# Graph layer with FFT convolution, one core: where the first four filter kinds of a batch are put, and when they are loaded

## The chip, the cores and the metric

The kernel runs on one core of a Trainium2 chip. The metric is the device time of one execution in microseconds (us). The engines are named as in the profile: PE multiplies matrices (PEld is its loading of weights, which overlaps), DVE is the vector engine, ACT the scalar engine, POOL the GpSimd engine, and SP the engine whose queue issues most of the DMA transfers. All times below are of this kernel's runs or of one profiled execution of it.

## The reference, cut to what matters

There are 64 graphs of 256 nodes with 256 features each. One layer is computed:

```python
h = relu(layernorm(x))                       # x: 64 x 256 x 256
xc = transpose(h)                            # channels x nodes
c = relu(bn1(conv1d(xc, conv1_w)))           # width 1
c = bn2(conv1d(c, conv2_w))                  # width 17, padded by 8
x_conv = transpose(relu(c + xc))
s = h @ w_se.T + b_se                        # 3 values per node
A = exp(-dist(s, s)) * adj
x_nmp = A @ relu(h @ w_msg.T + b_msg)
out = x + GRU(input=[x_conv, x_nmp], state=h)   # 256 features, gates r, z, n
```

The change concerns the filter of the convolution of width 17.

## The kernel before, in words

**Batches and pairs.** The 64 graphs are worked on as 32 pairs; four pairs make a batch, so there are eight batches (`NB`). In the loop over `b`, `i` is the first pair of the batch that is finished and `nxt` the first of the next one, which is prepared at the same time.

**The convolution.** The convolution of width 17 is done in a transformed domain. The transform of four pairs is made on DVE (`split`, `forward`), into tiles `U`, `V`, `PT`, `Sv`. In that domain the filter is 47 matrices of 256 x 256 numbers, called kinds here; a kind is named by a point `n` and a number 0, 1 or 2 (`TURNS` is their order). They are computed once, in the first batch, and written to device memory (`filt`). Every batch loads all 47 again, 256 KB each, into tiles `wb` of SBUF, of which there are nine (`SLOTS`). `product` takes the kind that stands first in the deque `WB` and issues four matmuls of 128 x 128 by 128 columns with it. `begin(m)` does the two products of number 0 for two points and has ACT copy the sum to the other half of the PSUM accumulator; `complete(m)` adds the products of numbers 1 and 2, and ACT copies the results to `Yv` or `Yu` (which is `V`). DVE then transforms back (`branch_back`, `odd_back`, `q_back`, `p_back`, `join`).

**Slots.** `free` holds the numbers of the free slots, `pending` the kinds still to load, and `load_kinds` pairs them, one DMA on SP's queue for each kind. After a product its slot goes back to `free` and new loads are recorded. When all 47 kinds are used, all nine slots are free; `roles` then takes all nine of them as work tiles for the gates (`ah`, `axn`, `axc`, `bh`, `bxn`, `bxc` for sums of operands, `e` for a partial product, `tz0` and `tz1` for the gate z). At the end of the batch seven come back by `give`, and `load_kinds` records the first seven loads of the next batch; `tz0` and `tz1` come back a little later in the next batch.

**The gates.** `gates(i)` does the GRU of one pair with `seven`, a product of 2 x 2 blocks by seven multiplications, once for the gates r and z and once for the two halves of gate n, with the function `between` recorded between the two. A batch has four gates, of `i` to `i + 3`, and the last ones run just ahead of the first products of the next batch. In the last gates the message of pair `nxt` (`message`, matmuls `aux<-w_msg,hT`, a DVE addition, small ACT copies to `Z`) is woven in. `embed` transposes `Z` on PE, and nine small ACT copies bring the result to `zT`. `affinity` makes the matrix A from it.

**The tiles concerned.** `adjh` (512 KB) takes the adjacency of a pair from device memory by four DMAs (`load_adj`); `join_adj` has ACT copy it to `adj_rows` in two instructions, one for each half of every number, after which `adjh` stands empty until the next `load_adj`. `xnms` is a ring of two tiles of 512 KB each; `aggregate(i)` writes one of them, and the gates of pair `i` read it last. `hh` and `halves` are the tiles through which the next pairs' `h` is transposed by DMA (`turn_h`, `sort_h`, `join_h`).

**What sets the order.** Every instruction is recorded (`Recorder`), with its dependences found from the elements that it reads and writes. `plan` then orders all engines' queues by a list schedule with costs and due times of its own, and `emit` issues them in that order. So the place where a call is written in the loop is not where its instruction stands in its engine's queue: a load is issued as soon as the planner thinks fit, once its tile's last reader is done. All instructions have the line of the recording helper, 371, in the profile; they are told apart by the names of their tiles, `out<-in`.

Of the kernel before, what the change touches and what calls it, by code (L numbers as in the profile page):

```python
# [13 lines left out]
FP = mybir.dt.float32  # L14
# [472 lines left out]
def kernel(  # L487
# [20 lines left out]
    B, N, D = x.shape  # L508
# [3 lines left out]
    NB = B // GB  # L512
    NP = B // G
    DC = D // P
# [26 lines left out]
    def keep(name, *dims):  # L541
        return const.tile([P, *dims], FP, name=name)
# [26 lines left out]
    SLOTS = 9  # L569
    WARM = 21  # L570
    slots = [keep(f"wb{k}", DC, D) for k in range(SLOTS)]
# [8 lines left out]
    adjh = keep("adjh", 2 * MC * W // 2).bitcast(U16).rearrange("p (k w) -> p k w", w=W)  # L580
# [59 lines left out]
    def join_adj(i):  # L640
        if not BY_DMA <= i < NP:
            return
        v = adj_rows.bitcast(U16).rearrange("p (g c) (n j) -> p j c g n", g=G, j=2)
        u = adjh.rearrange("p (c j) (g n) -> p j c g n", j=2, g=G)
        for j in range(2):
            nc.scalar.copy(v[:, j], u[:, j])
# [75 lines left out]
    p = aux()  # L722
# [175 lines left out]
    free = deque(range(SLOTS))  # L898
# [3 lines left out]
    def load_kinds(count=SLOTS):  # L902
        for _ in range(count):
            if not (free and pending):
                return
            n, kind = pending.popleft()
            WB.append((free.popleft(), n, kind))
            m, k = PLACE[n, kind]
            nc.sync.dma_start(out=slots[WB[-1][0]], in_=filt[m][:, k])


    def operands(n):
        if n < 8:
            c, h = n // 2 % 2, n // 4 * 2 + n % 2
            return Sv(c, h), V(c, 4 + h), V(c, h)
        if n < 12:
            c, h = (n - 8) // 2, n % 2
            return U(c, 4 + h), U(c, h), U(c, 2 + h)
        if n < 14:
            return U(n - 12, 6), PT(n - 12, 2), PT(n - 12, 3)  # L920
        if n == 14:
            return U(0, 7), PT(0, 1), PT(1, 1)
        return U(1, 7), PT(1, 0), None
# [3 lines left out]
    def product(p, n, kind, start):  # L927
        k, a, b = WB.popleft()
        assert (a, b) == (n, kind)
        for o in range(DC):  # L930
            for c in range(DC):
                mm(p[:, (n % 2 * DC + o) * P:(n % 2 * DC + o + 1) * P], slots[k][:, c, o * P:(o + 1) * P],
                   operands(n)[kind][:, c::DC, 0, :], start=start and not (o or c), stop=c == DC - 1,
                   skip_group_check=True)
        free.append(k)
        load_kinds(2)

    def begin(m):

        p = OPEN[m] = acc()  # L940
        for n in (2 * m, 2 * m + 1):
            product(p[:, 0], n, 0, n % 2 == 0)
        nc.scalar.copy(p[:, 1], p[:, 0])

    def complete(m):

        p = OPEN.pop(m)
        for kind in (1, 2):
            for n in (2 * m, 2 * m + 1):
                if operands(n)[kind] is not None:  # L950
                    product(p[:, 2 - kind], n, kind, False)
        re, im = (p[:, c].rearrange("p (n a e) -> p a n e", n=2, e=NW) for c in range(2))
        if m < 4:
            nc.scalar.copy(Yv(m % 2, m // 2 * 2, 2), re)
            nc.scalar.copy(Yv(m % 2, 4 + m // 2 * 2, 2), im)
        elif m < 6:
            nc.scalar.copy(Yu(m - 4, 0, 2), re)
            nc.scalar.copy(Yu(m - 4, 2, 2), im)
        elif m == 6:
            t = Yu.t[:, :, :, 6:8, :].rearrange("p a c n e -> p n a c e")  # L960
            nc.scalar.copy(t[:, 0], re)
            nc.scalar.copy(t[:, 1], im)
        else:
            nc.scalar.copy(Yu(0, 5)[:, :, 0], re[:, :, 0])
            nc.scalar.copy(Yu(1, 5)[:, :, 0], im[:, :, 0])
            nc.scalar.copy(Yu(1, 4)[:, :, 0], re[:, :, 1])
            nc.scalar.mul(Yu(0, 4)[:, :, 0], im[:, :, 1], 0.5)
# [14 lines left out]
    def message(i):  # L982
        if i >= NP:
            return
        for g in range(G):
            for c in range(MC):
                p = aux()
                for k in range(DC):
                    mm(p[:, :D + SE], chunk(HT[i][:, k], g, c), w_msg[:, k, :], start=(k == 0), stop=(k == DC - 1))
                nc.vector.tensor_add(msg_tile[:, g, c], p[:, :D + SE], b_msg)  # L990
        s = msg_tile[:, :, :, D:]
        flat = s.rearrange("p g c s -> p (g c) s")
        nc.scalar.mul(Z[:, 0, :, :SE], flat, -2.0)
        nc.scalar.activation(Z[:, 0, :, SE:2 * SE], flat, AF.Square)
        nc.scalar.copy(Z[:, 1, :, :SE], flat)
        nc.scalar.activation(Z[:, 1, :, 2 * SE:KD], flat, AF.Square)
        for g in range(G):
            nc.scalar.activation(msg_tile[:, g, :, :D], msg_tile[:, g, :, :D], AF.Relu)
# [179 lines left out]
    def gates(i, between=None):  # L1178
# [43 lines left out]
        if between:  # L1222
            between()
# [97 lines left out]
    for b in range(NB):  # L1321
# [26 lines left out]
        if b == 0:  # L1348
# [4 lines left out]
            xnms = Ring(late.tile([P, DC, W], FP, name=f"xnm{k}") for k in range(2))  # L1353
# [60 lines left out]
        def between():  # L1414
            affinity(i + 2)
            join_h(nxt + 1)
            stats(nxt + 2)
        gates(i, between)
        finish(i)
        for n in IN:  # L1420
# [10 lines left out]
        def between():  # L1431
            join_h(nxt + 2)
            join_adj(i + 3)
            message(i + 3)
            stats(nxt + 3)
        gates(i + 1, between)
        finish(i + 1)
        for n in IN:
# [29 lines left out]

        def between():
            join_adj(nxt)  # L1470
        gates(i + 3, between)
        message(nxt)
        if b == NB - 1:
# [50 lines left out]
```

## Time and profile before

| what | value |
|---|---|
| runs | 1688.8, 1692.25, 1693.15 us; median 1692.25 us |
| profiled execution | 1694.44 us, its span 1692.7 us |
| granted PE clock | 0.995 |
| busy, share of the span | PE 98%, PEld 84%, DVE 86%, ACT 67%, POOL 13% |
| loads `wb<-filt` | 376, 256 KB each, on SP's queue |
| loads `adjh<-halves_d` | 112, 128 KB each, on SP's queue |
| DMA moved in all | 261.37 MB, 154 GB/s over the span |

A timeline line gives the start in us, how long the merged group lasts, the engine, the operation with its tiles, the shape and the count of records, and in brackets the idle time ahead of it and what ended it. One matmul of this kernel's 4-byte numbers shows as two records on PE. SPq lines are the issues of DMAs by SP's queue.

### The profile page before, as it was taken

Reading aid. Unit: us, or ns where it says so; the run is one execution under the profiler, and the core shown is the slowest. Engines: PE = TensorE matmul, PEld = TensorE weight load, DVE = VectorE, ACT = ScalarE, POOL = GpSimd, SP = SyncE. Lnnn points to the kernel's source line nnn. Section 1 sums busy time; section 2 is a strip of 40 time slices with the busy share of each in tenths; the row PEclk is TensorE's granted clock in tenths of the full one; section 3 lists DMA queues with packets and bytes.
Section 4 is the critical chain, followed back from the end, with each engine's and each line's share of the span. In section 5 each row is a group of like instructions: output and inputs, shape, how many; then the busy total and the mean of one; then the engine's idle time right before and its main releaser. Section 6 shows DMA issues by size and latency. Waiting matters only on the chain.

```text
span 1692.7 us, 26271 instructions
## 1 busy us (share of the span) xinstructions
PE 1662.7 (98%) x8984; PEld 1420.2 (84%) x8984; DVE 1458.6 (86%) x3401; ACT 1133.6 (67%) x2029; POOL 227.9 (13%) x245
## 2 busy tenths in 40 slices
PE   9999999999999999999999999999999999999997
PEld 6888878988889788888889887898888978898886
DVE  7978989798898998898988988979988989789545
ACT  5545776686767767677665877578576776667554
POOL 4211010022010121102110031002211022000010
PEclk9999999999999999999999999999999999999999
DMA  9981566856568365784458645684646846376032
GB/s 240 304 275 61 128 123 160 276 138 128 111 199 235 94 131 112 229 210 97 116 119 270 166 97 117 159 270 111 142 109 204 225 100 131 82 237 144 13 58 55
DMA packets 314936, 261.37 MB, mean 154 GB/s; under 512 B 192875, under 2 KB 240263, under 8 KB 314802
## 3 DMA queue, kind: packets, MB, share of 16 engines
q1 hardware_dynamic: 297010, 216.71, 48.5%
q0 software_dynamic: 17376, 42.66, 11.2%
q8 instruction: 71, 1.16, 0.3%
q14 instruction: 63, 0.52, 0.1%
q10 hardware_dynamic: 416, 0.32, 0.1%
HBM read 156.60 MB, written 43.78 MB: 118 GB/s over the span
## 4 chain that ended last, share of the span: by engine, by line
PE 64%; DVE 29%; DMA 4%; issue 2%; ACT 2%; SPq 0%; DVEq 0%; ACTq 0%
PE acc L371 44%; PE aux L371 20%; DVE V L371 6%; DVE T L371 4%; DVE tr L371 4%; DVE U L371 3%; DVE wb L371 3%; DMA wb<-filt 3%; DVE gn L371 2%; DVE acc L371 2%; DVE Yv L371 1%; DVE PT L371 1%; DVE st L371 1%; DVE msg L371 1%; DMA hh<-halves 1%
## 5 line engine op out<-in xcount | busy, mean ns | idle before, releaser
L371 PE MATMUL acc<-wb,w_ih 128*128 128x256 f32 x768 | 191.9, 379 | 0.0
L371 PEld LDWEIGHTS acc<-wb,w_ih 128*128 128x128 f32 x768 | 146.0, 190 | 19.7
L371 POOL DMA_DIRECT2D back<-in_x_dram x62 | 56.8, 1056 | 750.8 <-ACT back L371 717.5
L371 POOL TENSOR_TENSOR rstd<-rstd,neg_half 128x4 f32<-128x4 f32 x32 | 84.8, 2650 | 455.4 <-DVE shift L371 266.4
L371 PE MATMUL aux<-wb,w_x 128*128 128x256 f32 x576 | 139.9, 384 | 2.5 <-ACT e L371 2.3
L371 PE MATMUL acc<-wb,w_x 128*128 128x256 f32 x576 | 136.2, 382 | 5.3 <-DVE acc L371 5.3
L371 DVE SCALAR_TENSOR_TENSOR V<-T,V 128x128 f32<-128x128 f32 (+2 forms) x448 | 139.9, 372 | 0.0
L371 ACT COPY back<-tr 128x512 uint16<-128x512 uint16 x124 | 128.0, 1077 | 15.2 <-DVE tr L371 14.9
L371 PEld LDWEIGHTS acc<-wb,w_x 128*128 128x128 f32 x576 | 108.0, 190 | 30.5 <-DVE acc L371 12.3
L371 PEld LDWEIGHTS aux<-wb,w_x 128*128 128x128 f32 x576 | 108.8, 191 | 22.1 <-ACT e L371 4.3
L371 PE MATMUL aux<-w_msg,hT 128*128 128x259 f32 x512 | 121.5, 381 | 0.0
L371 PEld LDWEIGHTS acc<-U,wb 128*128 128x128 f32 x1024 | 117.1, 192 | 2.9 <-DMA wb<-filt 1.1
L371 PE MATMUL acc<-U,wb 128*128 128x128 f32 x1024 | 117.6, 275 | 1.6 <-DMA wb<-filt 0.9
L371 PE MATMUL acc<-V,wb 128*128 128x128 f32 x1024 | 118.6, 275 | 0.0
L371 PEld LDWEIGHTS acc<-V,wb 128*128 128x128 f32 x1024 | 116.4, 192 | 0.7 <-DMA wb<-filt 0.3
L371 PE MATMUL acc<-wb,w_hh 128*128 128x256 f32 x384 | 110.1, 381 | 0.7 <-ACT acc L371 0.7
L371 ACT ACTIVATE gn<-acc,bn_columns 128x512 f32<-128x512 f32 (+1 forms) x64 | 43.5, 680 | 97.2 <-PE acc L371 85.6
L371 PEld LDWEIGHTS aux<-w_msg,hT 128*128 128x128 f32 x512 | 96.5, 190 | 14.2
L371 PE MATMUL acc<-Yv,w_ih 128*128 128x256 f32 x380 | 107.9, 379 | 0.1
L371 PE MATMUL aux<-hT,w_c 128*128 128x512 f32 x224 | 105.5, 593 | 0.8 <-DVE msg L371 0.8
L371 PE MATMUL aux<-e,msg 128*128 128x256 f32 x448 | 103.6, 380 | 0.0
L371 PE MATMUL acc<-hT,w_hh 128*128 128x256 f32 x380 | 103.5, 381 | 0.0
(196 smaller groups left out, 3885.6 us busy)
## 6 DMA issues: line engine op xcount, KB each, us to landing
wb<-filt SPq DMA_DIRECT2D x376, 256.0 KB
back<-in_x_dram POOLq DMA_DIRECT2D x62, 256.0 KB, 5.4
out_dram<-back POOLq DMA_DIRECT2D x62, 256.0 KB, 2.8
x<-in_x_dram SPq DMA_DIRECT2D x58, 256.0 KB
halves_d<-halves SPq DMA_DIRECT2D x28, 512.0 KB
adjh<-halves_d SPq DMA_DIRECT2D x112, 128.0 KB
hh<-halves SPq DMA_DIRECT2D x108, 128.0 KB
filt<-Yv SPq DMA_DIRECT2D x18, 224.0 KB
```

Source lines behind the costliest of these rows:

```text
L371: self.tasks.append(Task(engine, lambda: method(*args, **kw), cost, size, self.first))
```

## The change

In `between` of a batch's last gates, after `join_adj(nxt)` has been recorded, four more slots are appended to the nine: the two halves of `adjh`, and the two halves of that tile of the ring `xnms` that the next `aggregate` will write. `load_kinds` then records loads of the first four kinds of the next batch into them. After the product of a kind in such a slot the slot is not given back to `free`. The last batch does not do this. The kinds of the first four products are the same as before; the seven slots that `give` returns at the end of the batch take the next seven kinds. The next adjacency (`load_adj(i + 1)` of the next batch) can go into `adjh` only after the products of the first two kinds, since `adjh` holds these until then.

```diff
@@ product
-        free.append(k)
+        if k < SLOTS:
+            free.append(k)
         load_kinds(2)
@@ between, last gates of a batch
             join_adj(nxt)
+            if b + 1 < NB:
+                spare = [adjh.bitcast(FP).rearrange("p a n -> p (a n)").rearrange("p (k c d) -> p k c d", k=2, c=DC)[:, k]
+                         for k in range(2)]
+                t = xnms.tiles[(xnms.n + 1) % 2].rearrange("p c (k d) -> p (c k) d", d=D)
+                spare += [t[:, k * DC:(k + 1) * DC] for k in range(2)]
+                slots[SLOTS:] = spare
+                free.extend(range(SLOTS, SLOTS + len(spare)))
+                load_kinds()
         gates(i + 3, between)
```

## The prediction

> **What bounds the kernel now.** I read the page's busy shares first, then the PE's waits, then the busy time by stage around one change of batch (near 1,092 us; the other six look alike), then the timeline of PE and SP there.
>
> ```profile
> PE 1662.7 (98%) x8984; PEld 1420.2 (84%) x8984; DVE 1458.6 (86%) x3401; ACT 1133.6 (67%) x2029; POOL 227.9 (13%) x245
> PE acc L371 <- DVE acc L371: 5.3, 11, 1.1
> PE acc L371 <- DMA wb<-filt: 5.3, 8, 1.3
> ```
> PE is the bound. (The waits give us in total, times and the longest.) All its idle time is 30 us, and the waits for filter kinds are one of its two largest entries. Only an edit that takes bubbles out of PE's stream can pay.
>
> ```profile
> 1050.00:1092.00 42.00, 42.00 (x190) 35.59 (x189) 38.50 (x94) 25.33 (x35) 5.74 (x8) 1.00 0.56 116
> 1092.00:1124.00 32.00, 30.75 (x244) 29.22 (x243) 23.98 (x56) 23.76 (x48) 2.24 (x3) 1.00 0.92 295
> 1124.00:1160.00 36.00, 36.00 (x253) 32.12 (x252) 34.26 (x72) 27.96 (x60) 1.84 (x2) 1.00 0.83 212
> ```
> The columns after the length are busy PE, PEld, DVE, ACT, POOL, then clock, DMA share and GB/s. The gates (first row) keep PE full at 0.56 of the DMA engines; in the filter products (second row) the DMA engines are 0.92 busy and PE is not full.
>
> ```profile
> 1092.80 0.59 PE L371 MATMUL acc<-hT,w_x 128*128 128x256 f32 x2
> ...
> 1095.39 0.60 PE L371 MATMUL aux<-w_msg,hT 128*128 128x259 f32 x2
> 1095.83 1.05 PE L371 MATMUL acc<-Sv,wb 128*128 128x128 f32 x8
> 1098.13 2.94 PE L371 MATMUL acc<-Sv,wb 128*128 128x128 f32 x24 [1.25 <-DMA wb<-filt]
> 1100.91 3.74 PE L371 MATMUL acc<-V,wb 128*128 128x128 f32 x32
> ...
> 1110.16 0.71 PE L371 MATMUL aux<-zT 9*128 9x256 f32 x8
> ```
> ```profile
> 1077.13 0.93 SPq L371 DMA_DIRECT2D halves_d<-halves  x1
> 1092.13 28.22 SPq L371 DMA_DIRECT2D wb<-filt  x33
> 1120.44 3.53 SPq L371 DMA_TRANSPOSE halves<-hh  x1
> ```
> A matmul is two records, so eight records are one kind. Four kinds (x32) run from 1100.91 to 1104.49, so a kind takes 0.895 us of PE, and its 256 KB in that time are 293 GB/s: what the DMA engines deliver here at 0.92. The first load leaves at 1092.13 because the slots are in the gates' hands until then, 3.7 us ahead of the first product; the second kind comes 1.4 us late, and supply at par with demand never builds a lead.
>
> **What the Trainium skill says.** "Perfetto Trace Analysis", Optimization Strategy: the same gap repeating on the engine that should be saturated can mean that memory for the next tile is lacking; it agrees, all nine slots being occupied in the gates. "DMA: Bandwidth & Descriptors", Issuing engines are not separate DMA queues: all transfers interleave on 16 engines, so a move helps only into time in which these are free; 0.56 against 0.92 agrees. The same page, Specifications, gives some 358 GB/s of HBM per core; the trace shows 295 over the stage, so no reserve of supply is to be counted on.
>
> **The change, part by part.** The number of instructions is unchanged: 376 loads, 112 adjacency loads. Of the 47 kinds of each of seven batches four, 28 in all, are loaded early; the order in which every engine's queue stands after the first of them is planned anew, and I read it from the built program.
>
> *Bubbles removed.* From the first `hT,w_x` of a batch's last gates to the first double `zT` matmul, PE has six gate matmuls at 0.4325 (2.60), one late message matmul (0.43), 14 kinds at 0.895 (12.53) and two transposes (0.215): 15.78 us. Shown: 1110.16 - 1092.80 = 17.36, a bubble of 1.58. In the same way, with the extra matmuls that three of them have, the seven changes of batch give 0.91, 1.45, 1.57, 1.93, 1.58, 1.28, 0.87: 9.6 us. That is more than the 5.7 us that the idle column shows there, since matmul ends overlap. With four kinds in place (3.6 us of PE), PE need not wait at the start, and the other loads, still issued from about 1092.5, gain 3.6 us. A load every 0.87 us at 300 GB/s puts the fifth kind down by about 1096 for a use at 1099.6, the eleventh by about 1101 for 1105. So the second wait, twelve kinds in (at 505.99 and 507.67, 708.54, 908.33 in other batches), goes too: 1 MB less must arrive in the burst, against 256 KB of adjacency that come in.
>
> *What is late next.* The first product also needs the accumulator that ACT empties for the gates: its copy ends 2.66 us after that `hT,w_x`. The new order puts the last message matmul earlier and the two transposes in its place, so PE gets there at 2.60 + 0.21 = 2.81. The margin is 0.15 us and a hand-over is not shown; I allow 0.1 to 0.3 per batch, 0.7 to 2.1 in all, and take 1.4. The transposes in turn need the message's DVE addition and four small ACT copies (together under 1.5 us), which in the new order stand ahead of ACT's gate copies, in a stretch where ACT is idle 5.2 us: nothing. Five `zT` copies of 0.26 now stand before the copy that opens `complete(0)`: ACT gets to its end at 3.85 + 1.29 + 0.48 = 5.6, PE needs it at 2.81 + 4 x 0.895 = 6.4: nothing.
>
> *The early loads themselves.* Two (`adjh`) stand in SP's queue where the next adjacency was prefetched, near 1046; two (`xnm`) after the first `hh` piece, near 1063.5. These must wait for DVE's last `gn<-gn,xnm` (ends 1066.2), and three `hh` pieces and what follows queue behind: 2 us late with two issues of 0.32. ACT's join of `hh` at 1071.8 may then stand up to 1 us; ACT is idle 4.5 us at 1076.3, so nothing reaches PE. 1 MB at 0.56 DMA share is hidden.
>
> *Adjacency moved.* Four loads of 128 KB (0.575 us of SP each) lose their prefetch. Two now stand behind the seventh slot load and wait for the first two kinds' products (about 1097.8); the next load behind them needs a later product anyway: nothing. Two stand just ahead of the transpose at 1120.44 and delay it and the kinds behind it by 1.15 us; those kinds are used 7 us later. ACT joins the last pair between the copies of `begin(4)` and `begin(5)`, near 1125; the second copy isn't needed until `complete(5)`, near 1132. Nothing, unless the pair takes over 10 us to land (a load took 5.5: issued about 1092.6, awaited to 1098.1).
>
> *The re-planned order.* Its cost is not shown. The batch's length, `hT,w_x` to `hT,w_x`, is 199.07, 202.04, 199.43, 200.23, 199.44, 198.85: the same work in slightly different orders differs by up to 3 us. I bound it at -2.5 to +2.5 us for the seven together in the likeliest case and take +1, a loss, since a new order can meet DVE (95% busy in the third row above).
>
> *Sum.* 9.6 - 1.4 - 1.0 = 7.2, say 7 us, between 4 and 12. The profiled execution took 1694.44 us with a span of 1692.7; it becomes 1687.4. It stands 2.2 us over the median 1692.25, which becomes **1685.3**.
>
> **The rivals.** *The bubble becomes another wait (0.21).* PE still stops ahead of the first product, for ACT's copy out of the accumulator, or gains at the start and waits for DVE in the gates. For it: the profile already names ACT (`xnm`, `gn`) at three changes of batch. Against: that copy ends 0.37 us ahead of PE's start in the stretch above. Left over are 1 to 4 us: about 1689.8.
>
> *A worse order (0.13), slower.* One of the re-planned batches' orders becomes the repeating one and is like the batch of 202.04 us, with waits of 0.76 for DVE's `msg` and 1.14 for DVE's `acc`: 2.6 us over its neighbours. It decides from five such batches: 13 less 7, 6 us slower; all seven give 18 - 7 = 11, 1703. Against: six of seven orders in the trace are not like that.
>
> *Adjacency late (0.03), slower.* ACT stands in the last join until PE waits at `complete(5)`. It decides from 11 us of landing; 13 us in seven batches would cost 14, 7 more than the gain: 1699.
>
> *The loads do nothing (0.03).* If PE was held by ACT in all these stretches and the DMA named in the waits is not the last to come, nothing changes: 1692.
>
> **How the numbers follow.** The likeliest case (0.60) is 1685.3, its own range 1680 to 1688. A measurement of this kernel can tell about 0.3%, 5.1 us, from no change. Faster by more than that: nearly all of the likeliest and a little of the first rival, 0.62. Within it: most of the first and the last rival, 0.22. Slower: 0.16. The range 1679.5 to 1697 leaves out the slower cases (0.13 beyond its end) and 0.06 below.
>
> **What would show it.** In the changed profile, `acc<-Sv,adjh` and `acc<-Sv,xnm` follow the gates with under 0.3 us of idle; PE's wait for `wb<-filt` is under 1 us in all from the second batch on; the stretch from `hT,w_x` to the double `zT` falls from 17.4 to about 16; batches last about 198.5 us. Four products in place and a PE idle as before would prove the sum wrong at "what is late next"; batches over 200 with a clean start, at the re-planned order; SP or ACT waiting for `adjh` with PE behind, at the adjacency.

## The result, and the profile after

Five runs of the changed kernel have a median of 1679.42 us (1678.19 to 1683.27), five of the kernel before 1692.02 us (1688.8 to 1693.15). The ratio is 0.9936, with an interval of 0.9917 to 0.9955: faster, by more than the 0.3% that can be told here. The forecast was 1685.3 us, with a range of 1679.5 to 1697.

The profiled execution took 1678.21 us with a span of 1676.4, against 1694.44 and 1692.7. These 16.3 us are not all the change's. Up to the first `hT,w_x` of the last gates of batch 1, PE's order is the same in both programs, and that point lies at 287.42 us after and at 292.03 before: 4.6 us that the edit's work on PE cannot have made. (Over all the profiles shown below it lies between 285.1 and 292.0, whatever the kernel; in the second profile of each it is 290.62 after and 289.95 before. What it goes with is told in the last section.) The six batch lengths from there on add up to 1187.81 instead of 1199.06 us, 11.25 less, and the rest of the program differs by 0.4.

First the engines' busy shares and the loads of the slots, from the page; then PE's waits (us in total, times, the longest).

```profile
PE 1653.3 (99%) x8984; PEld 1418.2 (85%) x8984; DVE 1459.4 (87%) x3401; ACT 1135.1 (68%) x2029; POOL 233.8 (14%) x245
...
wb<-filt SPq DMA_DIRECT2D x348, 256.0 KB
```
```profile
PE acc L371 <- DVE acc L371: 5.0, 11, 0.7
...
PE acc L371 <- DMA wb<-filt: 0.6, 1, 0.6
```

PE has as many instructions as before, 8984. The slots take 348 loads instead of 376; the other 28 go into the new places. PE's wait for `wb<-filt` was 5.3 us in 8 times, of which one of 0.9 lies in the first batch. It is 0.6 in one, which lies at 112 us, also in the first batch, where the change does nothing. The wait for DVE's `acc`, the largest now, was there before with the same 11 times.

The next fence is the busy time by stage around the fifth change of batch, in the first two of the three stages whose rows of before were shown, which here lie 12.6 us earlier.

```profile
1037.40:1079.40 42.00, 42.00 (x191) 35.76 (x190) 38.93 (x95) 24.87 (x35) 5.73 (x8) 1.00 0.57 129
1079.40:1111.40 32.00, 32.00 (x259) 30.59 (x258) 25.79 (x59) 23.32 (x49) 2.32 (x3) 1.00 0.88 278
```

In the second row PE was busy 30.75 of 32 us and is now busy throughout. It gets through 259 records there, 15 more than before; DMA is down from 0.92 to 0.88 and from 295 to 278 GB/s. The first row's DMA share, where the early loads were added, rose only from 0.56 to 0.57, its rate from 116 to 129 GB/s: there was room for them. In the third stage PE is full as before, 36.00 of 36.

The timelines of PE, of SP and of ACT at that place follow.

```profile
1080.21 0.59 PE L371 MATMUL acc<-hT,w_x 128*128 128x256 f32 x2
...
1082.81 0.38 PE L371 MATMUL aux<-ident,z 128*128 128x128 f32 x2
1083.02 1.95 PE L371 MATMUL acc<-Sv,adjh 128*128 128x128 f32 x16
1084.81 1.95 PE L371 MATMUL acc<-Sv,xnm 128*128 128x128 f32 x16
1086.60 7.31 PE L371 MATMUL acc<-V,wb 128*128 128x128 f32 x64
1093.74 1.95 PE L371 MATMUL acc<-Sv,wb 128*128 128x128 f32 x16
1095.62 0.71 PE L371 MATMUL aux<-zT 9*128 9x256 f32 x8
```
```profile
1033.87 0.82 SPq L371 DMA_DIRECT2D adjh<-filt  x2
...
1052.68 0.92 SPq L371 DMA_DIRECT2D xnm<-filt  x2
1053.65 1.95 SPq L371 DMA_DIRECT2D hh<-halves  x3
...
1079.54 4.04 SPq L371 DMA_DIRECT2D wb<-filt  x7
1083.89 1.47 SPq L371 DMA_DIRECT2D adjh<-halves_d  x2
```
```profile
1082.29 0.58 ACT L371 COPY xnm<-acc 128x512 f32<-128x512 f32 x1
...
1085.29 0.57 ACT L371 COPY acc<-acc 128x512 f32<-128x512 f32 x1
```

The early loads leave 49 and 32 us ahead of their products, `adjh` at 1033.87 for 1083.02 and `xnm` at 1052.68 for 1084.81. The products follow the gates with no bracket, that is, no idle time: the stretch from `hT,w_x` to the double `zT` is 1095.62 - 1080.21 = 15.41 us. It was 17.36. Of the 1.95 us less, 0.43 is the last message matmul, which now stands ahead of the stretch; the rest is the bubble.

**A measure for all the kernels.** For the experiments I take each of the seven changes of batch from the first `hT,w_x` of the last gates to the first `aux<-e,msg` behind it, and subtract the matmuls that stand in it at their back-to-back times (0.21625 us for a record of 256 columns, 0.895 for a kind, 0.215 for the two transposes, 0.645 for the double `zT`). At a change with no gap this leaves 0.15, which I also subtract. What is left is called the bubble. (The expectations recorded ahead of the runs name it without this last subtraction, 1.05 us more over seven changes.) "Rest" is what the six batch lengths have outside these stretches, with the gates' and messages' matmuls counted into it: it shows what an order costs apart from the change of batch.

| kernel | early kinds, where | bubble in seven changes | six batch lengths | rest |
|---|---|---|---|---|
| before | none | 9.79 | 1199.06 | 1055.15 |
| before, another profile | none | 7.99 | 1196.25 | 1053.87 |
| `late` | the same tiles, late | 9.15 | 1194.38 | 1051.41 |
| `yv_one` | 1, `Yv` | 4.05 | 1194.51 | 1055.86 |
| `yv_two` | 2, `Yv` | 2.41 | 1190.83 | 1053.52 |
| `adjh_only` | 2, `adjh` | 2.21 | 1187.62 | 1050.86 |
| `xnm_only` | 2, `xnm` | 1.58 | 1189.56 | 1053.08 |
| `yv_four` | 4, `Yv` | 0.05 | 1187.71 | 1052.76 |
| `adjh_yv2` | 4, `adjh` and `Yv` | 4.26 (no wait: see there) | 1191.68 | 1052.64 |
| after | 4, `adjh` and `xnm` | 0.16 | 1187.81 | 1052.74 |
| after, another profile | 4, `adjh` and `xnm` | 0.71 | 1188.28 | 1052.67 |

All are in us and from one profiled execution each. From 285 to 1480 us the granted PE clock is 1.00 in every one of these eleven profiles, so the six batch lengths are compared at one clock.

One part of this bubble is not a wait. At the first change of batch of before, in both its profiles, the four `zT` matmuls stand in two groups with other products between them:

```profile
303.59 0.70 PE L371 MATMUL aux<-zT 9*128 9x256 f32 x4
...
309.78 0.70 PE L371 MATMUL aux<-zT 9*128 9x256 f32 x4
```

In `xnm_only` the first change has two groups too; in the changed kernel they are one group at all seven. `adjh_yv2` below, which has two groups and no wait, shows the price: 0.82 us. Taking it off, my estimate of what PE waits in the seven changes is 9.0 and 7.2 us for before and 0.8 for `xnm_only`.

### The profile page after: what moved, and what is told of

Its sections match the earlier page's. It is cut to its first block, busy times and chain, and to the rows that moved or that the text cites. A ratio compares the mean times of both kernels' runs of the same rounds, so it can differ in the third digit from the quotient of the medians.

```text
span 1676.4 us, 26283 instructions
## 1 busy us (share of the span) xinstructions
PE 1653.3 (99%) x8984; PEld 1418.2 (85%) x8984; DVE 1459.4 (87%) x3401; ACT 1135.1 (68%) x2029; POOL 233.8 (14%) x245
## 4 chain that ended last, share of the span: by engine, by line
PE 72%; DVE 24%; issue 2%; DMA 1%; ACT 1%; SPq 0%; DVEq 0%; ACTq 0%
PE acc L371 50%; PE aux L371 22%; DVE V L371 5%; DVE tr L371 3%; DVE T L371 3%; DVE U L371 3%; DVE wb L371 3%; DVE gn L371 2%; DVE acc L371 2%; DVE st L371 1%; DVE PT L371 1%; DMA wb<-filt 1%; DVE msg L371 1%; DVE Sv L371 0%; DVE Yv L371 0%
## 5 line engine op out<-in xcount | busy, mean ns | idle before, releaser
L371 PE MATMUL acc<-xnm,w_ih 128*128 128x256 f32 x380 | 103.2, 379 | 0.0
```

The lines of the kernel that those rows point to most:

```text
L371: self.tasks.append(Task(engine, lambda: method(*args, **kw), cost, size, self.first))
```

## The experiments

The lead theory is that kinds that are already there when PE reaches the first product are what takes the bubble away. Its rivals are that the order planned anew is what gains, with the loads' lead beside the point, and that the gain is partly paid back by what the loads push aside: the prefetch of the next adjacency out of `adjh`, and the queues behind the `xnm` loads.

### The same loads in the same tiles, issued late (`late`)

```diff
@@ seven
         part(E[:, 0], 7, i, unit)
+        MARK[0] = nc.last["tensor"]
@@ end of a batch
         gates(i + 3, between)
+        (the block with spare, moved here out of between)
+        nc.behind = MARK[0]
+        load_kinds()
+        nc.behind = None
```

The four extra slots exist and are used as in the changed kernel, but the loads into them must stand behind a marked matmul of the last gates, near the place where the first load left before.

> The same spare tiles as in the changed kernel, the same loss of the adjacency's prefetch, and a newly planned order; but the four loads are made to wait for the product of the last gates that frees the first work slots (near 1092 us of the kernel before), so that they leave no earlier than the first load did before. Theory lead (PE stood because no load could leave before the gates gave the slots up): the bubbles of 9.6 us come back, 1688 to 1693 us, PE's wait for wb<-filt, adjh<-filt and xnm<-filt 4 us or more. Theory order (the gain came from the re-planned queues, or from having more slots): 1679 to 1683 us and hardly any such wait.

Measured: 1689.97 us, the median of 22 runs, beside 1691.84 for 57 of before in the same group of runs, a ratio of 0.9995 (0.9982 to 1.0009): no gain that can be told. PE's timeline, SP's, and PE's waits:

```profile
1084.98 1.04 PE L371 MATMUL aux<-w_msg,hT 128*128 128x259 f32 x4
1087.65 2.02 PE L371 MATMUL acc<-Sv,adjh 128*128 128x128 f32 x16 [1.63 <-ACT gn L371]
1089.51 1.95 PE L371 MATMUL acc<-Sv,xnm 128*128 128x128 f32 x16
```
```profile
1081.72 0.85 SPq L371 DMA_DIRECT2D wb<-filt  x2
1082.61 0.91 SPq L371 DMA_DIRECT2D adjh<-filt  x2
1083.56 0.98 SPq L371 DMA_DIRECT2D xnm<-filt  x2
```
```profile
PE acc L371 <- ACT gn L371: 3.1, 2, 1.6
...
PE acc L371 <- DMA adjh<-filt: 2.5, 4, 1.0
```

The products of `adjh` and `xnm` stand first, as in the changed kernel, but their loads leave at 1082.61, 5 us ahead, and PE stands 1.63 us. (They leave 0.22 us after the first `hT,w_x`, at 1082.39; in before the first load left 0.67 us ahead of it, so `late` gives a little less lead than before has.) The bubble is 9.15 us, within what before shows. The wait is named after the load in some places and after ACT's `gn` in others, and the name is only that of the event that the profile saw last. ACT isn't what holds PE: at the change near 887 us the first product starts at 887.51, before the same `gn` (887.74 to 888.46), and in the changed kernel PE goes on 0.15 us behind ACT's first copy out of the accumulator, which here ends at 1085.05, 2.6 us ahead of the product. The tiles and a new order alone don't take the bubble away: the lead does.

The new order is not without effect, though. The rest of `late` is 1051.41, without before's long second batch, which is 1.6 to 3.0 us longer than its neighbours, and its lengths are 1.9 to 4.7 us shorter than before's two. In the ratio of all the runs this can't be told from nothing.

### Two kinds each: `adjh_only` and `xnm_only`

```diff
@@ between (adjh_only)
+                spare = spare[:2]
@@ between (xnm_only)
+                spare = spare[2:]
                 slots[SLOTS:] = spare
```

> Only the two kinds in adjh are loaded early, the two in the xnm tile are not. Theory lead: two kinds are 1.8 us of PE, enough for the first wait (1.1 to 1.4 us) but not for all of the second, so about two thirds of the gain: 1682 to 1685 us. Theory order: 1679 to 1682 us, as with four. If a single early kind were enough because only the first landing is late: the same as with four.

> Only the two kinds in the xnm tile are loaded early; adjh keeps its prefetch of the adjacency. Theory lead: as adjh_only, 1682 to 1685 us, and the difference between the two is the price of the lost adjacency prefetch, which I put at 0 to 1 us. Rival (the adjacency's four loads in the filter burst cost time in the changed kernel): clearly below adjh_only, by 2 us or more.

Measured: `adjh_only` 1679.18 us (10 runs, ratio 0.9939, 0.9921 to 0.9957), `xnm_only` 1683.57 us (17 runs, 0.9957, 0.9944 to 0.9970). Either half alone takes most of the bubble away: 2.21 and 1.58 us are left, where two kinds are 1.8 us of PE time, more than nearly every one of before's bubbles. By its time alone, `adjh_only` came out as expected if the order were the cause, and `xnm_only` as expected of the lead; the profiles part the two, for the bubbles fall alike, and of the 4.4 us between the medians 2.2 are found in the rest. `adjh_only` loses the adjacency's prefetch and is yet the shorter, so no price of that loss shows. About half of what is left of `adjh_only`, 1.06 us, stands in one place, the second wait that the prediction spoke of, twelve kinds in. This is its timeline, with both kinds of the early pair and the kinds ahead of the double `zT`:

```profile
882.73 1.95 PE L371 MATMUL acc<-Sv,adjh 128*128 128x128 f32 x16
884.51 1.95 PE L371 MATMUL acc<-Sv,wb 128*128 128x128 f32 x16
...
894.64 2.02 PE L371 MATMUL acc<-Sv,wb 128*128 128x128 f32 x16 [0.81 <-DMA wb<-filt]
```

The start is clean; at 894.64 the supply falls short once. That is what the third and fourth kind are for, and by the bubbles it is worth a microsecond or two in all. `adjh_only` has the shortest rest of all, 175.13 us in five of its six batches against 175.4 in three of the changed kernel's and 1.9 us less over the six, so it ends level with it: 1679.18 beside 1679.07 of a larger sample of the changed kernel below. Two kinds in `adjh` are as good as four; which is the better can't be told. Why these orders differ by 0.3 us a batch is open.

### The same four kinds in other tiles (`yv_four`)

```diff
@@ between
-                spare = [adjh ... for k in range(2)]
-                t = xnms.tiles[...]
-                spare += [t[...] for k in range(2)]
+                spare = [xcv(j, o).rearrange("p (c d) -> p c d", c=DC) for j in range(2) for o in range(DC)]
```

The kinds go into the parts of `Yv` that belong to the batch's first two pairs, whose gates are done. `adjh` keeps its prefetch of the next adjacency, and the free tile of the ring `xnms` stays empty.

> Four kinds early as in the changed kernel, but in four blocks of Yv that the gates of the batch's first two pairs have read for the last time; adjh and the xnm tiles are left alone, so the adjacency keeps its prefetch and SP's queue does not wait for DVE's last read of xnm. Theory lead: the same bubbles gone, 1678 to 1682 us, the same as the changed kernel. Rival (the displaced adjacency loads and the waiting xnm loads cost something): 2 us or more below the changed kernel. Rival order: anything from 1679 to 1692 us, and the bubbles need not go.

Measured: 1682.49 us (21 runs), ratio 0.9953 (0.9942 to 0.9965).

```profile
887.70 0.60 PE L371 MATMUL aux<-w_msg,hT 128*128 128x259 f32 x2
888.14 3.73 PE L371 MATMUL acc<-Sv,Yv 128*128 128x128 f32 x32
891.71 3.74 PE L371 MATMUL acc<-V,wb 128*128 128x128 f32 x32
```

PE's timeline shows all four kinds in one unbroken run behind the message. The bubble is 0.05 us and the batch lengths 1187.71, where the changed kernel has 1187.81. Other tiles, another order, the same gain in these lengths: it doesn't hang on `adjh` or `xnms`, and the displaced adjacency prefetch has no price that they show. The median lies 0.5 us above what was expected of the lead, and the interval of its ratio overlaps the changed kernel's (0.9942, below).

### Both kernels once more (`before_again`, `after_again`)

The programs are those of before and after, for a second profile of each and more runs.

> The kernel before, profiled once more, to see what of its trace repeats. By stretch: from the first hT,w_x of a batch's last gates to the first e,msg, PE stood 10.8 us longer than its matmuls need over the seven changes of batch; expected again, 9.5 to 11. The rest of the batches: one of six was 2.9 us longer than the others (178.2 against 175.1 to 175.4). If that comes from the planned order, it repeats in the same batch; if from that execution, it does not, and the rest of the batches is about 1052 us as in the changed kernel. The 292.0 us up to the first stretch belong to work that the change leaves alone; where they differ from run to run they follow the granted clock, 285 to 292 us.

> The changed kernel once more, for more executions of it beside the kernel before. Its first five gave 12.6 us less. If the gain is the bubble of 9.6 us and the rest was the clock of few executions and one long batch of the profiled one, more runs give 8.5 to 10.5 us less, about 1682 us; if the re-planned order gives 3 us beside it, 12 to 13 us less, 1679 us.

Measured: the changed kernel 1679.07 us (six runs, 1675.93 to 1684.13), before 1690.12 (19 runs, 1685.75 to 1694.22), ratio 0.9942 (0.9927 to 0.9957): 9.8 us by the ratio. The second profile of before, whose execution took 1690.94 us, waits for the same thing, in other batches and amounts (two of the ten, 1.1 us, in the first batch):

```profile
PE acc L371 <- DMA wb<-filt: 4.6, 10, 0.8
```

Its bubble is 7.99 us where the first profile has 9.79, less than was expected (8.5 to 10 in this measure), and its second batch is again the longest in the rest, 177.07 us (178.16 in the first profile, 175.1 to 175.9 for the other batches). So the long batch belongs to before's order, and its size varies. The changed kernel repeats better: 1188.28 and 1187.81. Its second profile has one wait for `wb<-filt` behind the first batch, 0.33 us at 902.93, fifteen kinds in.

The spread of the medians follows the clock granted to PE. Over the 90 runs of before beside the experiments, those at 0.997 have a mean of 1687.1 us (12 runs), those at 0.995 1690.4 (21), those at 0.993 1694.3 (11). The changed kernel has 1678.6 at 0.997 (4) and 1683.6 at 0.993 (2). At equal clock the gain is about 8.5 and 10.7 us. In the first comparison, with 12.6 us between the medians, three of the five changed runs had 0.997. The clocks of the five of before are not on record, so that the clock gave the surplus is likely and not shown.

### Fewer kinds in the same place (`yv_one`, `yv_two`)

```diff
@@ between
-  ... for j in range(2) for o in range(DC)]
+  ... for j in range(2) for o in range(DC)][:1]   (yv_one; [:2] in yv_two)
```

> One kind loaded early, into a block of Yv; adjh and xnm are left alone. Theory lead: each early kind gives 0.9 us of lead at each change of batch; one leaves about 1.55 - 0.9 = 0.65 us of bubble each, 4 to 6 us over the seven by the measure in which the kernel before has 10.8 and the changed one 1.2. Theory slots (any kind in place lets the burst start in time): 1 to 3 us.

> Two kinds loaded early, into Yv; the adjacency keeps its prefetch. Beside adjh_only, which loads as many and loses it. If the displaced adjacency costs nothing: the same as adjh_only within 1.5 us, 1679 to 1682 us, bubble 2 to 3.5 us in all. If adjh_only's left-over bubble of 3 us comes from the adjacency's loads in the burst: bubble 1 to 1.5 us and 1 to 2 us less time. Theory lead with two kinds being too few for the second wait: the bubble stays at 3.

Measured: `yv_one` 1690.52 us (one run, at a clock of 0.993), `yv_two` 1682.33 us (14 runs, ratio 0.9958, 0.9947 to 0.9970). PE's wait for the slots in `yv_one`, of which two, 0.9 us, lie in the first batch:

```profile
PE acc L371 <- DMA wb<-filt: 1.4, 4, 0.7
```

The bubble goes with the number of kinds: 8.0 to 9.8 us with none, 4.05 with one, 2.41 with two, 0.05 with four. For one and two these are 5.1 and 3.5 in the measure of the expectations, in the ranges that were given for the lead. One kind, 0.895 us of PE, at seven changes should take off 6.3 us at most; it took 4 to 6, or 3 to 5 without the split `zT` group of before's first change. The order of `yv_one` keeps before's long second batch (178.32 us of rest). Its one run is 3.7 us below before's mean at that clock, which a single run can't tell from chance. `yv_two` beside `adjh_only` is a second comparison for the adjacency: the one keeps the prefetch, the other loses it, and the one that loses it has the shorter rest by 2.7 us.

### Four kinds, two in `adjh` and two in `Yv` (`adjh_yv2`)

```diff
@@ between
-                t = xnms.tiles[...]
-                spare += [t[...] for k in range(2)]
+                spare += [xcv(0, o).rearrange("p (c d) -> p c d", c=DC) for o in range(DC)]
```

This was to be a better version than both, with the early kinds of `yv_four` and the short rest of `adjh_only`.

> Four kinds early, two in adjh as in the changed kernel and two in Yv in place of the xnm tile, so that SP's queue does not wait for DVE's last read of xnm. Theory lead: the bubble of four kinds, 1.1 to 1.8 us over the seven changes of batch (adjh_only with two kinds has 3.05). The rest of six batches is set by the order that the planner makes: adjh_only's was 1050.9, the changed kernel's 1052.7. If both come together: 1186 us for the six batches, 1 to 2 us less than the changed kernel, 1677 to 1679 us; if the order goes back to the changed kernel's, the same as it.

Measured: 1684.59 us (9 runs), beside 1692.39 for 14 of before in the same group, ratio 0.9953 (0.9938 to 0.9969). It has neither: the rest is 1052.64, as with four kinds elsewhere, and each of the five inner changes of batch is 0.82 us longer than its matmuls. PE's timeline shows where:

```profile
888.57 1.95 PE L371 MATMUL acc<-Sv,adjh 128*128 128x128 f32 x16
890.36 1.95 PE L371 MATMUL acc<-Sv,Yv 128*128 128x128 f32 x16
...
900.49 0.70 PE L371 MATMUL aux<-zT 9*128 9x256 f32 x4
901.12 1.16 PE L371 MATMUL acc<-Sv,wb 128*128 128x128 f32 x8
902.21 0.70 PE L371 MATMUL aux<-zT 9*128 9x256 f32 x4
902.84 2.05 PE L371 MATMUL acc<-Sv,wb 128*128 128x128 f32 x16
```

The kinds are there and PE has no idle time. But the planned order has split the four `zT` matmuls: in the changed kernel they are one group of eight records and take 0.645 us until the next matmul (1095.62 to about 1096.27), here two groups of four, 901.12 - 900.49 and 902.84 - 902.21, 0.63 us each. That is 0.615 us more PE time in a batch. The kind between the groups takes 902.21 - 901.12 = 1.09 us in place of 0.895, which makes up the 0.82. A price of the order, then, and not a wait.

## Why the prediction was right, and where its sizes were off

**The mechanism was right.** What was to show it did: no idle time ahead of `Sv,adjh` and `Sv,xnm`; no wait for `wb<-filt` from the second batch on in the first profile and one of 0.33 us in the second; the stretch at 15.4 us in the five inner changes, from which a message matmul of 0.43 has gone, and 16.3 in the first and last, where "about 16" was named; batches of 197.1 to 198.8 us for "about 198.5". `late` took the lead away and the bubble came back, `yv_four` brought the gain with other tiles. The reading from the Trainium skill's "Perfetto Trace Analysis", Optimization Strategy, that the repeated gap can mean lacking memory for the next tile, is borne out: four places of 256 KB closed it. The step that rests on the same skill's "DMA: Bandwidth & Descriptors", Issuing engines are not separate DMA queues, fits: the early loads went into a stage with the DMA engines at 0.57, and the later stage fell from 0.92 to 0.88. That the place of the loads had to be one with free DMA engines no run here shows, since none put them early into a busy one.

**Bubbles removed, 9.6 us.** The measure above gives 9.8 for the same profile and 8.0 for the second one of before; the first was a profile with long bubbles, and the mean of the two is 8.9, of which about 0.8 is the split `zT` group of the first change and not a wait. (The prediction's sum took that group's first half as work.) The figure was near, but that it varies by 1.8 us from one execution to the next was not reckoned with.

**What is late next, 1.4 us allowed.** The two readings were exact: PE reaches the first product at 1083.02 - 1080.21 = 2.81, and ACT's copy of the accumulator ends at 1082.29 + 0.58 - 1080.21 = 2.66. That margin of 0.15 us was enough, and no hand-over beyond it had to be paid: the bubble left is 0.16 us in one profile and 0.71 in the other, and 0.6 of the 0.71 is at the one change with the late kind at 902.93. The term was too large by 0.7 to 1.2 us, and what is left of it is supply, not ACT. The second copy ends at 5.65 after `hT,w_x`, needed at 6.39: as worked out.

**The early loads and the adjacency, nothing.** They stand where they were put, at 1033.87 and 1052.68 (1046 and 1063.5 less the 12.6 us by which all lies earlier are 1033.4 and 1050.9), with the three `hh` pieces behind the second pair. No wait of PE or of ACT in PE's path came of it, and `yv_four` and `yv_two`, which leave the adjacency alone, are not faster.

**The re-planned order, +1 us taken as a loss.** This is the term that was furthest off, and with the wrong sign. The rest of the six batches is 1054.5 us in the mean of before's two profiles and 1052.7 in the two of after: 1.8 us of gain, within the bounds of 2.5 that were given. It comes from before's second batch, 178.2 and 177.1 us where after has 175.6 in both its profiles. In the timeline of before's first profile that batch has PE idle at these places:

```profile
557.37 1.98 PE L371 MATMUL aux<-hT,w_c 128*128 128x512 f32 x4 [0.76 <-DVE msg L371]
...
641.52 2.86 PE L371 MATMUL acc<-wb,w_x 128*128 128x256 f32 x12 [1.14 <-DVE acc L371]
```

The second profile of before has no idle time at the first of these places and the same 1.14 us at the second, which goes with its shorter batch; the changed kernel has none at the first and 0.67 at the second. The prediction saw this batch and held it up as what a new order might bring; it could as well have been read as what a new order would most likely remove, since six of seven orders didn't have it.

**The sum.** Predicted: 9.6 - 1.4 - 1.0 = 7.2. By the two profiles of each kernel: the six batch lengths have a mean of 1197.65 before and 1188.05 after, 9.6 us less. By the larger comparison, 9.8. Of the 9.6, 7.8 us are the bubbles of the first six changes, with about 0.8 for the `zT` group that is no longer split, and 1.8 the rest. The last change's bubble, 0.6 us, does not show behind them: the remainder of the program is as long as before within 0.2 in the means, at clocks that differ there from profile to profile. The forecast was 2.6 us short of 9.8 because the two terms taken as losses, 1.4 and 1.0, came out as about 0.4 and as a gain of 1.8, while the bubbles were 0.7 shorter than 9.6. The first comparison's 12.6 us lie beyond the 4 to 12 that were named, and its median, 1679.42, 0.1 us below the named range; by its ratio, 0.9936 of 1692.25, it is 1681.4 and inside. The larger comparison's 9.8 us lies inside 4 to 12. The rival of a wait in the place of the old one left at most 0.7 us; those of a worse order and of a late adjacency did not come.

## What to carry to other kernels

Here weights were used about as fast as they came (293 GB/s in the products, 295 moved in that stage), and a start without lead was still felt twelve kinds later. The cure was a few buffers filled before: look for tiles that stand empty just then, and take only as many as the bubble is long, since here two kinds of 0.895 us did nearly all that four did. An edit to a kernel whose order is planned by a program comes with a new order, so give it a gain as well as a loss, and look whether the old order has a batch that is out of line. Take a second profile of the same program before summing up its bubbles.

## What was not expected of the hardware

Four matmuls with 9 rows each, whose operands start 32 partitions apart, take 0.645 us together, and two of them 0.63: half of the group saves next to nothing. The Trainium skill's "TensorE: Matmul & The Clock Gate", Part 3: Packing small matmuls, says that matmuls of few rows on different row groups can run at the same time; the 0.645 us for four, where one matmul of 256 columns takes 0.4325, agree. The runs add that it pays to keep such a group together: splitting it cost 0.615 us, and 0.82 with the matmuls between.

Programs with the same beginning take differently long over it from run to run: the first stretch, the same PE instructions in the same order in all these kernels, took 285 to 292 us. These 7 us are 0.4% of the whole and more than half of the gain that was to be measured. They go with the granted clock of this stretch: the one profile with 1.00 in all of it (`xnm_only`) took 285.1 us, the four with 0.99 between 70 and 285 us (`late`, `adjh_only`, `after`, `yv_two`) 286.0 to 287.6, the four with 0.98 there 289.9 to 290.9, and the two with 0.98 from the start on (before's first, `yv_one`) 292.0. From 285 to 1480 us all have 1.00. To compare two kernels by their profiles, take the stretch where the clock is the same.
